# A graph attention layer on one core: a 23rd key-and-value buffer, and the running of the segment maxima one step later

## The chip, the core and the metric

The kernel runs on one core of a Trainium2 chip. A core has five instruction queues that run side by side[...]: TensorE (PE in the profile, with its weight loads as PEld), VectorE (DVE), ScalarE (ACT), GpSimd (POOL) and SyncE (SP, which here only issues DMAs). The metric is device time in microseconds (us) of one launch; lower is better.

## The reference

There are 3125 nodes with 128 features, and 100,000 edges, sorted by destination, each of one of 5 types. For every type r the edges of that type attend, per destination node and head (8 heads of 16):

```python
logits = (q * k).sum(-1) / scale + attn_bias[r][None, :]
masked_logits = jnp.where(mask[:, None], logits, NEG)
max_v = jax.ops.segment_max(masked_logits, dst, num_segments=n)
exp_l = jnp.where(mask[:, None], jnp.exp(masked_logits - max_v[dst]), 0.0)
sum_exp = jax.ops.segment_sum(exp_l, dst, num_segments=n)
attn = exp_l / (sum_exp[dst] + 1e-12)
out = out + jax.ops.segment_sum(attn[:, :, None] * v, dst, num_segments=n)
```

Here q comes from the destination's features, k and v from the source's, with weights of the type. The sum over the types goes through an output projection, is added to the features and normalised, added to the features once more and normalised again.

## The kernel before

**Tables.** A prologue (about the first 120 us) multiplies the features with the weights of keys and values of all types and stores them in DRAM as `kv_d`, one row of 256 floats per node and type. Queries go to `q_d`, three bf16 parts each.

**Groups and steps.** The edges are cut into 196 groups of 512 (4 tiles of 128). A group's edges touch at most 25 consecutive nodes, so 125 rows of node and type. The main loop runs over steps k. In a step, group k goes through the first half of the work (logits), and an older group v, 16 to 19 steps behind (19 from v = 22 on), goes through the second half (softmax weights and sums). Keys and values of a group stay in SBUF in between: `kvs_[g % KVB]`, with KVB = 22 buffers of 4 KB per partition.

**The loop's operations**, by the names in the code and the line that the profile shows:

- `gather(g)` (L681, POOL): four indirect DMAs, each fetching 128 rows of `kv_d`. It is called AHEAD = 2 steps before the group's logits: in step k for group k + 2. It writes the buffer that group k + 2 - 22 read last in `weigh`.
- `spread_q` (L746, PE): one-hot matrix `hot` times the queries, 12 bf16 matmuls. `logits` (L759 product, L760 sum, DVE); `store_logits` (L765, SP) puts them in `lg_d`. `spot` (L737, DVE) makes `hot` for a later group from `kt`, which `fetch_keys` (L367, SP) brings; `fetch_q` (L373, SP) brings `qw`. Both are issued three steps ahead.
- `fetch_m` (L853, SP) brings the maxima `mw` of group v; `spread_m` (L863, PE) spreads them over the edges, into `me`; `less_max` (L872, DVE) subtracts; `exps` (L876, ACT); `weigh` (L881, DVE) multiplies the values; `weights` (L889, ACT); `sums` (L915, L917, L924, PE) adds up per node and type; `norm` (L936 to L939, DVE) divides.

On DVE the order within step k is `weigh(v)`, `less_max` of the next v, `norm`, `logits(k)`, `spot`, then parts of queries, maxima, projection and norms where they are due. On PE it is `spread_m` of the next v, `sums`, `spread_q(k+1)`. Each queue runs strictly in this written order.

**The maxima.** Nodes are handled in blocks of 128 (25 blocks, about 8 steps apart). `full_step[b]` is the step after whose logits all edges of block b have theirs; `ready[b]` is 8 steps later for whole blocks (7 for the last, smaller one), and is the first step in which a group of block b may be in its second half. In between:

- step ready - 7: `maxima_load` (L772, POOL), an indirect DMA from `lg_d` into `ell`. It waits for the last `store_logits` of the block to have landed, and gathers stand behind it in POOL's queue.
- steps ready - 6, - 5 and - 4, at the end of the step on DVE: `maxima` in three parts, for types 0 and 1, 2 and 3, and 4 (L795, L805, L810, L816; with the last part L821 to L831). The first part begins with an ACT copy `by_head` (L787). The last, smaller block does all in one part at ready - 4.
- step ready - 3, early in the step on SP: `store_m` (L839), into `m_d`.
- step ready - 2: the first two `fetch_m` of the block (L853), which wait for that store.
- step ready - 1: PE's `spread_m` of the block's first group.

Every engine's program is in the order in which the Python calls are made (`tc.manual_schedule()`), and the waits follow from which buffers are written and read.

Of the kernel before, what the change touches and what calls it, by code (L numbers as in the profile page):

```python
# [59 lines left out]
SB = P * E // N // SR  # L60
SPAD = 5
QB = 3
KVB = 22
HELD = 21
KVA = 9

# [63 lines left out]
NM = len(MB)  # L130


def windowed_path(
# [539 lines left out]
    ps = ctx.enter_context(tc.tile_pool(name="ps", bufs=2, space=PSUM))  # L673
    buffers(i for i in range(KVB) if i not in at_once)
    hold = ctx.enter_context(tc.tile_pool(name="hold", bufs=HELD))
    flow = ctx.enter_context(tc.tile_pool(name="flow", bufs=2))
    late_flow = ctx.enter_context(tc.tile_pool(name="late_flow", bufs=2))
    def gather(g):
        kv = kvs_[g % KVB]
        for t in range(T):  # L680
# [75 lines left out]
    def logits(g):  # L756
        kv, lg = kvs_[g % KVB], live["lg", g]
        prod = flow.tile([P, T, H], F32, name="prod", bufs=1)
# [20 lines left out]
    def maxima(b, c0, c1):  # L779

        whole = MB[b][2] is None
        nh = HEADS if whole else HEADS // 2
        if c0 == 0:
            ell = live.pop(("ell", b))
            by_head = ps.tile([P, HEADS, D], F32, name="by_head", bufs=1)[:, :nh]
            if whole:
                nc.scalar.copy(by_head, ell[:, :, :HEADS].rearrange("p s k -> p k s"))  # L787
            else:
                for h in range(2):
                    at = slice(h * P // 2, (h + 1) * P // 2)  # L790
                    nc.scalar.copy(
                        by_head[at], ell[at, :, h * nh : (h + 1) * nh].rearrange("p s k -> p k s")
                    )
            mine = late_flow.tile([P, D], F32, name="mine", bufs=1)
            nc.vector.scalar_tensor_tensor(  # L795
                mine, slot, deg[:, b : b + 1], ell[:, :, HEADS], op0=ALU.is_lt, op1=ALU.mult
            )
            mx = late_flow.tile([P, R, HEADS], F32, name="mx", bufs=1)
            mx = mx.rearrange("p r k -> p (r k)")[:, : R * nh].rearrange("p (r k) -> p r k", k=nh)
            live["max", b] = by_head, mine, mx  # L800
        by_head, mine, mx = live["max", b]
        n = c1 - c0
        shut = late_flow.tile([P, R, D], F32, name="shut", bufs=1)
        for r in range(c0, c1):
            nc.vector.tensor_scalar(  # L805
                shut[:, r - c0, :], mine, float(r + 1), -BIG, op0=ALU.not_equal, op1=ALU.mult
            )
        wl = late_flow.tile([P, RH * HEADS, D], F32, name="wl", tag="wl", bufs=1)
        wl = wl[:, : n * nh].rearrange("p (r k) s -> p r k s", k=nh)
        nc.vector.tensor_tensor(  # L810
            wl,
            by_head[:, None].to_broadcast([P, n, nh, D]),
            shut[:, :n, None, :].to_broadcast([P, n, nh, D]),
            op=ALU.add,
        )
        nc.vector.tensor_reduce(mx[:, c0:c1], wl, AX.X, ALU.max)  # L816
        if c1 < R:
            return
        live.pop(("max", b))
        bias = bias4 if whole else bias_h  # L820
        nc.vector.tensor_tensor(mx, mx, bias, op=ALU.add)  # L821
        nc.vector.scalar_tensor_tensor(mx, mx, NEG4, bias, op0=ALU.max, op1=ALU.subtract)
        m3 = late_flow.tile([P, R, 2, 3, HEADS // 2], BF16, name="m3")
        if whole:
            mxs = mx.rearrange("p r (h k) -> p r h k", h=2)
        else:
            m3, mxs = m3[:, :, :1], mx[:, :, None, :]
        nc.vector.tensor_copy(m3[:, :, :, 0, :], mxs)
        nc.vector.tensor_tensor(mxs, mxs, m3[:, :, :, 0, :], op=ALU.subtract)
        nc.vector.tensor_copy(m3[:, :, :, 1, :], mxs)  # L830
        nc.vector.tensor_tensor(m3[:, :, :, 2, :], mxs, m3[:, :, :, 1, :], op=ALU.subtract)  # L831
        live["m3", b] = m3

    def store_m(b):
        n0, n1, part = MB[b]
        m3 = live.pop(("m3", b))
        to = m_d[n0 * R : (n0 + (P if part is None else P // 2)) * R, :]
        if part is None:
            nc.sync.dma_start(  # L839
                to.rearrange("(p r) c -> p (r c)", r=R), m3.rearrange("p r h s k -> p (r h s k)")  # L840
            )
        else:
            to = to.rearrange("(p r) (h c) -> h p r c", r=R, h=2)
            for h in range(2):
                nc.sync.dma_start(
                    to[h],
                    m3[h * P // 2 : (h + 1) * P // 2, :, 0].rearrange("p r s k -> p r (s k)"),
                )
# [176 lines left out]
    def lag(b):  # L1025

        return LAG if MB[b][2] is None else LAG_H

    full_step = [step_of[full_at(n, D)] for n in MEND]
    ready = [full_step[b] + lag(b) for b in range(NM)]  # L1030


    at_k, k = {}, 0
    for v in range(NGR):
        k = max(k + 1, ready[block_of(v, MEND)])
# [26 lines left out]
    for k in range(-2, root_at[NT] + 2):  # L1062
        v, g = v_at.get(k), group_at.get(k)
        q_step = {k - f: b for b, f in enumerate(q_from) if b >= QB and -2 <= k - f <= 5}

        if k >= 0 and k + 3 in group_at:
            fetch_keys(group_at[k + 3])
            fetch_q(group_at[k + 3])
        if -2 in q_step:
            fetch_x("xq", q_step[-2])  # L1070
        for b in range(NT):
            if done_at[b] - 1 == k:
                fetch_x("xr", b)
            if norm_at[b + 1] + 1 == k:
                store_z(b)
        for b in range(NM):
            if ready[b] - 3 == k:
                store_m(b)
        if 5 in q_step:
            store_q(q_step[5])  # L1080
        for u in range(NGR):
            if max(at_k[u] - 3, ready[block_of(u, MEND)] - 2) == k:
                fetch_m(u)

        while gathered < NGR - 1 and step_of[gathered + 1] <= k + (AHEAD if k < final - 16 else 1):
            gathered += 1
            gather(gathered)
        for b in range(NM):
            if full_step[b] + 1 == k:
                maxima_load(b)  # L1090

        for b in range(NT):
            if done_at[b] + 1 == k:
                residual(b)
        if v_at.get(k - 4) is not None:
            by_node(v_at[k - 4])
        if v_at.get(k - 2) is not None:
            carry(v_at[k - 2])
        if 1 in q_step:
            turned(q_step[1])  # L1100
        if 3 in q_step or 4 in q_step:
            second_part()
        if 2 in q_step or 3 in q_step:
            first_part()

        if v_at.get(k + 1) is not None:
            spread_m(v_at[k + 1], 8 if k + 1 in group_at else 12)
        if v_at.get(k - 1) is not None or v_at.get(k - 3) is not None:
            sums(v_at.get(k - 1), v_at.get(k - 3))
        if k + 1 in group_at:  # L1110
            spread_q(group_at[k + 1])

        if v is not None:
            weigh(v)
        if v_at.get(k + 1) is not None:
            less_max(v_at[k + 1])
            exps(v_at[k + 1])
        if v is not None:
            weights(v)
        if k + 1 in group_at:  # L1120
            types(group_at[k + 1])
        if v_at.get(k - 2) is not None:
            norm(v_at[k - 2])
        if g is not None:
            logits(g)
            store_logits(g)
        if k + 2 in group_at:
            spot(group_at[k + 2])
        if v_at.get(k + 1) is not None:
            places(v_at[k + 1], 2 if k >= final - 1 else 0)  # L1130
        if 3 in q_step or 4 in q_step:
            third_part()
        if 2 in q_step or 3 in q_step:
            remainder()
        for b in range(NM):
            whole = MB[b][2] is None
            if ready[b] - 6 == k and whole:
                maxima(b, 0, 2)
            if ready[b] - 5 == k and whole:
                maxima(b, 2, 4)  # L1140
            if ready[b] - 4 == k:
                maxima(b, 4 if whole else 0, R)
        for b in range(NT):
            if done_at[b] == k:
                project(b)
        for b in range(NT + 1):
            if root_at[b] == k:
                roots(b)
            if norm_at[b] == k:
                norms(b)  # L1150
        if 0 in q_step:
            turn_q(q_step[0])
        if 1 in q_step:
            queries(q_step[1], 0, RH)
        if 2 in q_step:
            queries(q_step[2], RH, R)
# [505 lines left out]
```

## Time and profile before

| what | value |
|---|---|
| three runs | 1645.75, 1625.92, 1644.51 us; median 1644.51 |
| the profiled execution's own time | 1596.71 us |
| its span in the profile | 1594.9 us |
| busy: PE, DVE, ACT, POOL | 978.5, 931.1, 636.1, 797.2 us |
| mean granted TensorE clock | 0.707 |
| DMA moved | 203.63 MB, 128 GB/s |
| eight steps (one block of nodes) in the middle of the loop | about 57 us |

No engine is busy for more than 61% of the span. Busy time is an average: the loop's steps are held up by waits, and the rows that name these waits are in the prediction. In the page's groups the columns are: line, engine, operation, what is written and read, count, busy us, mean ns, and the idle time of the engine just before these instructions with who ended most of it. "remote" stands for a release that the profile cannot name, "issue" for time in which the engine waited for nothing that the profile shows. Matmul ends are modelled; when a matmul was really done shows in when the engine that waits for it goes on.

### The profile page before, as it was taken

To read this page: it belongs to the slowest core of one execution; us is meant where nothing else is said; L and a number is where in the kernel's file an instruction comes from. 1 tells how busy PE (TensorE), PEld (TensorE's weight loads), DVE (VectorE), ACT (ScalarE), POOL (GpSimd) and SP (SyncE) were. 2 spreads that over 40 slices of the span, in tenths; PEclk is the share of its full clock that TensorE was granted. 3 is DMA by queue.
4 is the path that set the end of the run, shared out by engine and by line. 5 is a ranking of instruction groups with operands and counts; after the bars stand their busy time and mean duration, and the time that the engine had idled before them with its cause. 6 is when DMAs were issued, how large, how long until landed. Compare 5 with 4: busy or idle time off the path is not lost. (4 is left out here: it accounts for less than half of the span.)

```text
span 1594.9 us, 25686 instructions
## 1 busy us (share of the span) xinstructions
PE 978.5 (61%) x7526; PEld 752.9 (47%) x7526; DVE 931.1 (58%) x2559; ACT 636.1 (40%) x2248; POOL 797.2 (50%) x901
## 2 busy tenths in 40 slices
PE   7931423655676676667566657566676556565786
PEld 3520322434555554555454545455555444454664
DVE  5521623645756656656655656556665665664786
ACT  2620121324434444443453444343444344344454
POOL 3455446254555555555555555555555555455400
PEclk9965556766777767777776777676777777767678
DMA  6963634444545545555554554455555455444410
GB/s 191 357 195 97 153 85 128 103 109 122 139 120 128 144 121 121 138 131 122 119 132 105 133 136 121 117 133 123 129 138 133 111 138 134 111 127 119 102 27 15
DMA packets 180889, 203.63 MB, mean 128 GB/s; under 512 B 83207, under 2 KB 146083, under 8 KB 180620
## 3 DMA queue, kind: packets, MB, share of 16 engines
q0 software_dynamic: 40896, 113.39, 25.4%
q1 hardware_dynamic: 135414, 83.80, 23.4%
q10 hardware_dynamic: 4430, 4.71, 1.2%
q8 instruction: 63, 1.03, 0.3%
q14 instruction: 86, 0.70, 0.2%
HBM read 166.50 MB, written 35.28 MB: 127 GB/s over the span
## 5 line engine op out<-in xcount | busy, mean ns | idle before, releaser
L681 POOL DMA_INDIRECT kv<-kv_d,idx x784 | 742.5, 947 | 534.3 <-DVE den L936 252.9
L915 PE MATMUL pp<-wv,at 128*125 128x136 f32 x1568 | 399.6, 386 | 68.3 <-issue 62.1
L915 PEld LDWEIGHTS pp<-wv,at 128*125 128x125 f32 x1568 | 298.1, 256 | 154.8 <-issue 149.9
L746 PE MATMUL qe<-qw,hot 125*128 125x128 bf16 x2352 | 235.3, 261 | 139.9 <-issue 69.1
L863 PE MATMUL me<-mw,hot 125*128 125x64 bf16 (+1 forms) x2352 | 150.4, 217 | 237.5 <-issue 112.2
L746 PEld LDWEIGHTS <-hot 125*128 125x128 bf16 x2352 | 207.9, 127 | 158.4 <-issue 89.0
L872 DVE TENSOR_TENSOR me<-lg,me 128x32 f32<-128x32 f32 x196 | 37.8, 193 | 395.8 <-remote 247.0
L863 PEld LDWEIGHTS <-hot 125*128 125x128 bf16 x2352 | 130.9, 114 | 264.6 <-issue 232.9
L876 ACT ACTIVATE me<-me 128x32 f32<-128x32 f32 x196 | 35.7, 182 | 511.7 <-DVE me L872 318.6
L901 ACT ACTIVATE at<-row_at,nkey 128x125 f32<-128x125 f32 x744 | 237.5, 398 | 0.0
L759 DVE TENSOR_TENSOR prod<-kv,qe 128x512 f32<-128x512 f32 x196 | 132.8, 678 | 83.2 <-remote 62.1
L881 DVE TENSOR_TENSOR wv<-kv,me 128x512 f32<-128x512 f32 x196 | 132.8, 677 | 42.1 <-remote 32.6
L760 DVE TENSOR_REDUCE lg<-prod 128x32 f32<-128x512 f32 x196 | 134.4, 686 | 6.7
L904 ACT ACTIVATE at<-at 128x500 f32<-128x500 f32 (+1 forms) x196 | 117.4, 599 | 6.2
L917 PE MATMUL pp<-pt,carried 125*5 125x136 f32 x390 | 100.4, 346 | 30.7 <-issue 16.3
L707 PE MATMUL prq<-wq,xTq 128*128 128x384 f32 (+1 forms) x88 | 48.5, 639 | 81.0 <-DVE rem L717 59.9
L772 POOL DMA_INDIRECT ell<-lg_d,start_i x25 | 23.6, 945 | 149.1 <-DMA lg_d<-lg 52.4
L924 PEld LDWEIGHTS pp<-rsum,o 125*128 125x128 f32 x392 | 84.0, 258 | 18.7 <-issue 18.1
L949 ACT COPY oT<-pp 128x25 f32 x196 | 33.7, 172 | 135.9 <-remote 89.1
L810 DVE TENSOR_TENSOR wl<-by_head,shut 128x1024 f32<-128x1024 f32 (+2 forms) x73 | 76.9, 1053 | 17.2 <-issue 10.3
L924 PE MATMUL pp<-rsum,o 125*128 125x25 f32 x392 | 74.4, 270 | 18.3 <-issue 13.7
L816 DVE TENSOR_REDUCE mx<-wl 128x16 f32<-128x1024 f32 (+2 forms) x73 | 76.5, 1048 | 2.5
(184 smaller groups left out, 1018.6 us busy)
## 6 DMA issues: line engine op xcount, KB each, us to landing
kt<-key_d SPq DMA_DIRECT2D x196, 128.0 KB
qw<-q_d SPq DMA_DIRECT2D x196, 96.0 KB
kv_d<-kvs SPq DMA_DIRECT2D x24, 640.0 KB
kv<-kv_d,idx POOLq DMA_INDIRECT x784
q_d<-q SPq DMA_DIRECT2D x22, 480.0 KB
lg_d<-lg SPq DMA_DIRECT2D x196, 18.0 KB
mw<-m_d SPq DMA_DIRECT2D x196, 6.0 KB
xr<-in_x SPq DMA_DIRECT2D x24, 64.0 KB
```

What stands on the lines that cost most here:

```text
L681: nc.gpsimd.indirect_dma_start(out=kv[:, t, :], out_offset=None, in_=kv_d[:, :], in_offset=bass.IndirectOffsetOnAxis(ap=idx[:, t, g : g + ...
L746: nc.tensor.matmul(qe[:, t, :], hot[:, t, :], qw[:WR, s, :], start=(s == 0), stop=(s == 2))
L759: nc.vector.tensor_tensor(prod, kv[:, :, :H], live.pop(("qe", g)), op=ALU.mult)
L760: nc.vector.tensor_reduce(lg[:, :, :HEADS], prod.rearrange("p t (k d) -> p t k d", d=HD), AX.X, ALU.add)
L810: nc.vector.tensor_tensor(wl, by_head[:, None].to_broadcast([P, n, nh, D]), shut[:, :n, None, :].to_broadcast([P, n, nh, D]), op=ALU.add,)
L863: nc.tensor.matmul(me[:, t], hot[:, t, :], mw[:WR, None, :, s, :].to_broadcast([WR, times, 2, HEADS // 2]), start=(s == 0), stop=(s == 2),)
L881: nc.vector.tensor_tensor(wv[:, :, :H].rearrange("p t (k d) -> p t k d", d=HD), kv[:, :, H:].rearrange("p t (k d) -> p t k d", d=HD), live ...
L901: nc.scalar.activation(at[:, t, :], row_at[:, :WR], AF.Abs, bias=nkey[:, t, g : g + 1], scale=1.0)
L904: nc.scalar.activation(at[:, on_dve:], at[:, on_dve:], AF.Relu, bias=1.0, scale=-1.0)
L915: nc.tensor.matmul(pp, at[:, t, :], wv[:, t, :], start=(t == 0), stop=(t == T - 1))
L917: nc.tensor.matmul(pp[:R], carried[:WR, g, :], live.pop(("pt", g - 1)), start=False, stop=False,)
L924: nc.tensor.matmul(op, live.pop(("o5", done)), rsum[:WR], start=True, stop=True)
```

## The change

The number of buffers goes from 22 to 23, with AHEAD unchanged at 2. `last` is the step of a block's last part of the maxima: ready - 3 for whole blocks, ready - 4 as it was for the smaller one. The parts run in `last` - 2, `last` - 1 and `last`, so one step later than before for whole blocks. `store_m` is called right behind the last part, at the end of that step, where it was called early in step ready - 3. `maxima_load` (ready - 7) and `fetch_m` (ready - 2 at the earliest) stay where they were.

```diff
-KVB = 22
+KVB = 23
...
-        for b in range(NM):
-            if ready[b] - 3 == k:
-                store_m(b)
...
         for b in range(NM):
             whole = MB[b][2] is None
-            if ready[b] - 6 == k and whole:
+            last = ready[b] - (3 if whole else 4)
+            if last - 2 == k and whole:
                 maxima(b, 0, 2)
-            if ready[b] - 5 == k and whole:
+            if last - 1 == k and whole:
                 maxima(b, 2, 4)
-            if ready[b] - 4 == k:
+            if last == k:
                 maxima(b, 4 if whole else 0, R)
+                store_m(b)
```

## The prediction

> **What bounds the kernel now.** I read the groups first, for who waits for whom. Columns after the bar: busy us, mean ns, then idle time before with its releasers.
>
> ```profile
> L681 POOL DMA_INDIRECT kv<-kv_d,idx x784 | 742.5, 947 | 534.3 <-DVE den L936 252.9
> L872 DVE TENSOR_TENSOR me<-lg,me 128x32 f32<-128x32 f32 x196 | 37.8, 193 | 395.8 <-remote 247.0
> L863 PE MATMUL me<-mw,hot 125*128 125x64 bf16 (+1 forms) x2352 | 150.4, 217 | 237.5 <-issue 112.2
> L772 POOL DMA_INDIRECT ell<-lg_d,start_i x25 | 23.6, 945 | 149.1 <-DMA lg_d<-lg 52.4
> ```
>
> DVE's great idle time stands in front of `less_max`, 395.8 of its 664 idle us: it waits for PE's `spread_m`. POOL's 534.3 us in front of gathers are waits for a buffer, released by DVE. DVE hardly waits for gathers: between the last issue of a group's gather and its product (L759) lie 12 to 26 us in steps 42 to 177 (I took the difference of the two rows for each group).
>
> Why does PE keep `less_max` waiting? The timeline (start us, duration) of POOL and of DVE early in the loop shows it most plainly:
>
> ```profile
> 242.88 0.94 POOL L772 DMA_INDIRECT ell<-lg_d,start_i  x1 [22.59 <-DMA lg_d<-lg]
> 245.91 0.94 POOL L681 DMA_INDIRECT kv<-kv_d,idx  x1 [2.09 <-issue]
> ...
> 279.66 0.94 POOL L681 DMA_INDIRECT kv<-kv_d,idx  x1 [0.30 <-issue]
> 291.70 0.94 POOL L681 DMA_INDIRECT kv<-kv_d,idx  x1 [11.09 <-DVE den L936]
> ```
>
> ```profile
> 260.16 0.69 DVE L881 TENSOR_TENSOR wv<-kv,me 128x512 f32<-128x512 f32 x1 [3.29 <-remote]
> 285.51 0.20 DVE L872 TENSOR_TENSOR me<-lg,me 128x32 f32<-128x32 f32 x1 [24.66 <-remote]
> ```
>
> From 245.9 to 280.6 POOL issues 28 gathers without a pause, 1.25 us each; DVE stands from 261 until 285.5, when PE has at last delivered. In the middle of the loop it is the same on a smaller scale:
>
> ```profile
> 680.05 0.68 DVE L881 TENSOR_TENSOR wv<-kv,me 128x512 f32<-128x512 f32 x1
> 683.42 0.68 DVE L881 TENSOR_TENSOR wv<-kv,me 128x512 f32<-128x512 f32 x1
> 691.03 0.20 DVE L872 TENSOR_TENSOR me<-lg,me 128x32 f32<-128x32 f32 x1 [6.93 <-remote]
> ```
>
> ```profile
> 681.00 0.94 POOL L681 DMA_INDIRECT kv<-kv_d,idx  x1 [3.90 <-DVE den L936]
> ...
> 689.75 0.95 POOL L681 DMA_INDIRECT kv<-kv_d,idx  x1 [0.30 <-issue]
> 695.29 0.94 POOL L681 DMA_INDIRECT kv<-kv_d,idx  x1 [4.59 <-DVE den L936]
> ```
>
> Two `weigh` free two buffers, POOL gathers two groups from 681.0 to 690.7, and `less_max` goes on at 691.03, 0.3 us after the last of them. So a step costs the 5 us of its gathers, in which PE delivers little after the first one or two us, and some 2.2 us in which PE and DVE catch up. A typical block of eight steps is 57.2 us: 40 of gathers, 1.25 for `ell`, 16 of POOL's pauses. I call the time in which PE delivers nothing the freeze; the trace does not say by what way a gather causes it.
>
> A rule of the Trainium skill speaks against this reading: "Trainium Architecture — The Big Picture", section "What this means for kernel authors", holds the engines for independent processors that delay one another through semaphores alone. `spread_m` waits for no gather. By the rule a longer run of gathers costs nothing, and the sum below would be -4 us at most. I go by the rows. Another, "Perfetto Trace Analysis", section "Optimization Strategy", says that a gap repeating on the engine that should be saturated can mean too few buffers. That reading of the 534.3 us would promise a gain from buffer 23; with 12 us of lead at least, POOL isn't that engine, and I put its worth at nothing.
>
> **Buffer 23.** The same 784 gathers of 0.947 us, no instruction added. `gather` in step k now needs the `weigh` of step k - 2, not k - 1. In steady running one `weigh` still frees one group. What changes is the meeting with `ell` once a block: POOL comes to it a step earlier, waits longer, and then finds three groups freed at once. I walk one block with the durations of 680 to 725, step 78 (third part included, see below) to 84, where the logits of step 81 close a block.
> - Before: `weigh` of 78 and 79 at 680.05 and 683.42; gathers to 690.7; `weigh` of 80 and 81 at 694.34 and 699.00; gathers 695.29 to 704.97; `less_max` of 81 at 706.08; `ell` 710.49; `weigh` of 83 at 711.47; gathers 711.74 to 721.44; `weigh` of 84 at 723.29, 1.85 after their end.
> - After: `weigh` of 78 at 680.05 frees a group, 681.0 to 685.7. Step 78 now holds the third part of the maxima, 3.0 us, so `weigh` of 79 is at 686.6 and frees the next, 687.6 to 692.3; that of 80, at about 690.3, the third, to 697.0. POOL then stands at `ell`, and nothing freezes: `less_max` of 80 about 697.8, `weigh` of 81 701.6, product of 81 703.1 (before 706.8), `ell` 3.7 later as before, 706.8, `weigh` of 83 at 707.7. Three groups are free: gathers from 708.0 to 723.0, where two ended at 721.44. `weigh` of 84 follows 1.85 later, 724.9 against 723.29.
>
> So DVE is 3.7 us ahead at `ell` and loses it all in the longer run: +1.6 us a block. The trace also has a stretch with that slack: steps 26 to 42, whose groups have a lag of 18 and not 19. From product 26 to product 42 it takes 120.6 us (305.5 to 426.1), and its `ell` waits 11.2 and 14.4 us, against 0.3 to 5.9 later. Two typical blocks take 114.4: +3.1 us a block. Against it stand steps 178 to 194, with one step of AHEAD and so the same slack: 105.6 us, but without new queries. That bounds it below, at about -3. I take +1.8, near the walk: 19 blocks from step 42, **+34**.
>
> **The maxima one step later.** Per block the same four L810/L816 pairs of 0.7 to 1.23 us and the tail L821 to L831, some 8.5 us, in other steps of DVE. The step in which the norms are due (717.1 to 722.2 in the timeline) loses 3.4 us of maxima; that time lay in a freeze, so it returns nothing. In the last of the three steps 3.0 us come before the next `weigh`; the walk has that. What waits for `ell` now is small: 10.2 us before `by_head` and 8.5 before `mine` in the whole run. A step later they are gone; half lies elsewhere hidden: **-4**.
>
> **The store at the end.** One DMA of 30 KB per block on SP. Before, it stood ahead of step ready - 3's `store_logits`; now SP waits for DVE's third part, about 3.7 us behind the `store_logits`. Behind it are queued the next `fetch_keys` and `fetch_q` (used 13 us after issue, covered) and the first two `fetch_m`. SP needs 3.4 us from the first of these to the first `mw` (682.97 to 686.38), and PE's weight load follows 2.55 us later. So `mw` comes some 4 us later: 692.9 in the walk, while `less_max` of 80 is held to 697.8 by gathers. Without that cover PE would wait 2.6 to 4 us a block. At the end of the loop there are no gathers left to cover it, and steps are short: two blocks, **+5**.
>
> Sum: 34 - 4 + 5 = +35 on 1596.71, or 2.2%. The profiled execution is 2.9% faster than the median of the runs, so I carry the ratio over: 1644.5 x 1.022 = **1680**.
>
> **Rivals.**
> - *Faster: more gathers under DVE work.* A single group's run beside a step with 5 to 6 us of DVE work costs POOL only a 0.93 us pause (the row at step 84), where runs of two cost 4.4 for two (my mean over 31 of them). Norms and maxima no longer share a step, so four steps of a block could cover a group, not three. Two more such groups save 2 x 1.3 us a block, 21 blocks: -55 us, 3.4%: 1588. It decides if the runs stay single; against it, the longer wait at `ell` makes runs of three.
> - *No change.* The time gained before `ell` and lost behind it are equal, as blocks of 52 and 63 us that follow each other already show: 1640 to 1650.
> - *Clearly slower: the maxima's store.* If the freeze ends before `mw` lands, PE waits up to 4.2 us in each of 22 blocks: +92 us, 1740. For it: in 10 of 22 blocks the first `spread_m` starts right behind its weight load, so `mw` is what came last. Against: DVE needs its result 3.3 us later.
>
> **The numbers.** A measurement of this kernel can tell about 2%. Forecast (slower by 2 to 4.5%, its own range 1660 to 1715) 0.33; no change 0.32; faster 0.25; clearly slower 0.10. So faster 0.25, same 0.32, slower 0.43. The range takes in half of the faster case and most of the slow one: 1600 to 1735.
>
> **What would show it.** `ell`'s idle time grows from 149 us to some 230 and is released by the store of the logits; gathers come in runs of 12 behind it; `less_max` keeps 380 to 430 us of idle time; PE's waits for `mw` stay below 40 us. I am wrong if POOL's runs become single and `less_max` waits under 330, or if `less_max` no longer follows the end of a run.

## The result and the profile after

| what | before | after |
|---|---|---|
| median of the runs | 1645.13 us (1625.92 to 1645.93, 4 runs) | 1742.81 us (1739.17 to 1749.28, 4 runs) |
| profiled execution | 1596.71 us | 1749.28 us |
| product of step 0 to that of step 42 | 304.1 us | 314.6 us |
| steps 42 to 178 | 982.0 us | 1100.2 us |
| steps 178 to 195, and from there to the end | 111.9 and 74.8 us | 128.9 and 78.3 us |

The ratio is 1.0656 with a 95% interval of 1.0603 to 1.0709: slower by 6.6%. The execution of the kernel before that left the trace, 1596.71 us, was faster than any of its four runs, so the two traces lie 153 us apart where the medians lie 98. They show where the time went, but make its amounts too large. Nearly all of it lies in the loop, and 118 us in its middle, where a block of eight steps grew from 57.8 to 64.7 us.

The rows of the groups after the change, columns as before:

```profile
L681 POOL DMA_INDIRECT kv<-kv_d,idx x784 | 745.1, 950 | 511.3 <-issue 225.9
L872 DVE TENSOR_TENSOR me<-lg,me 128x32 f32<-128x32 f32 x196 | 37.7, 192 | 547.9 <-remote 410.1
L863 PE MATMUL me<-mw,hot 125*128 125x64 bf16 (+1 forms) x2352 | 139.6, 219 | 186.6 <-ACT wv L889 72.5
L772 POOL DMA_INDIRECT ell<-lg_d,start_i x25 | 23.6, 943 | 318.4 <-DMA lg_d<-lg 146.3
```

The operations of POOL and DVE in these rows kept their length. POOL's idle time before `ell` more than doubled (149.1 to 318.4 us), and DVE waits 152 us more in front of `less_max` (395.8 to 547.9), about as much as the span grew. The timeline of one block shows how the two belong together. DVE first, `weigh` (L881) and `less_max` (L872):

```profile
565.03 0.65 DVE L881 TENSOR_TENSOR wv<-kv,me 128x512 f32<-128x512 f32 x1
...
567.91 0.68 DVE L881 TENSOR_TENSOR wv<-kv,me 128x512 f32<-128x512 f32 x1
...
570.82 0.68 DVE L881 TENSOR_TENSOR wv<-kv,me 128x512 f32<-128x512 f32 x1
...
576.49 0.68 DVE L881 TENSOR_TENSOR wv<-kv,me 128x512 f32<-128x512 f32 x1
595.75 0.20 DVE L872 TENSOR_TENSOR me<-lg,me 128x32 f32<-128x32 f32 x1 [18.59 <-remote]
```

And POOL in the same stretch:

```profile
571.51 0.94 POOL L772 DMA_INDIRECT ell<-lg_d,start_i  x1 [12.08 <-DMA lg_d<-lg]
572.76 0.95 POOL L681 DMA_INDIRECT kv<-kv_d,idx  x1 [0.30 <-issue]
...
591.53 0.95 POOL L681 DMA_INDIRECT kv<-kv_d,idx  x1 [0.30 <-issue]
602.50 0.95 POOL L681 DMA_INDIRECT kv<-kv_d,idx  x1 [10.02 <-DVE den L936]
```

POOL stands at `ell` for 12 us, up to 571.5. No gather runs, so DVE steps at 2.9 us a step and sets one buffer free with each `weigh`. When `ell` is out, POOL finds three groups free; the fourth `weigh` (576.49) is done 4.4 us after the first of their gathers has started. So POOL issues 16 gathers in 20 us, and the next one waits for the `weigh` behind them (602.5). `less_max` waits 18.6 us during that run and goes on 3.3 us after its last gather. Between steps 42 and 178 there are 17 such runs of four groups, one per block; before there was none (52 runs of one group, 41 of two, one of three; after 40, 14 and 17 of four. I join groups whose gathers follow each other within 0.8 us). All 17 stand right behind `ell`. In each of them DVE starts exactly one `weigh`, as it does in each of the 14 runs of two: a run twice as long brings DVE no further.

What PE does meanwhile, its matmuls in order of time:

```profile
577.33 0.33 PE L746 MATMUL qe<-qw,hot 125*128 125x128 bf16 x3
578.00 0.22 PE L746 MATMUL qe<-qw,hot 125*128 125x128 bf16 x1 [0.34 <-issue]
579.41 0.27 PE L746 MATMUL qe<-qw,hot 125*128 125x128 bf16 x1 [1.20 <-issue]
580.87 0.26 PE L746 MATMUL qe<-qw,hot 125*128 125x128 bf16 x1 [1.19 <-issue]
...
589.34 0.26 PE L746 MATMUL qe<-qw,hot 125*128 125x128 bf16 x1 [1.14 <-issue]
591.43 0.27 PE L746 MATMUL qe<-qw,hot 125*128 125x128 bf16 x1 [1.83 <-issue]
```

One `spread_q`, twelve matmuls that otherwise take 0.8 us, is drawn out over 14 us. Most of its matmuls start 1.4 us apart or a multiple of 0.7, with a weight load half-way between; the profile has no releaser for them ("issue"). So the freeze of the prediction is visible: PE waits for nothing that the profile shows, and crawls.

The crawl in these records is not the whole of it. Counted through the run, the `spread_m` that `less_max` waits for at 595.75 is this one:

```profile
574.39 0.52 PE L863 MATMUL me<-mw,hot 125*128 125x64 bf16 x12
```

It stands ahead of the crawl, and DVE got its result some 21 us after its modelled end. Whether PE works further behind than its records say, or the result was done and reached DVE late, no run shows.

### The profile page after: what moved, and what is told of

It is laid out like the page before. It is cut to its first block, busy times and chain, and to the rows that moved or that the text cites. A ratio compares the mean times of both kernels' runs of the same rounds, so it can differ in the third digit from the quotient of the medians.

```text
span 1747.5 us, 25673 instructions
## 1 busy us (share of the span) xinstructions
PE 988.0 (57%) x7526; PEld 749.7 (43%) x7526; DVE 928.0 (53%) x2559; ACT 629.9 (36%) x2248; POOL 799.9 (46%) x901
## 4 chain that ended last, share of the span: by engine, by line
DVE 26%; another core or an unknown queue 25%; PE 19%; issue 15%; ACT 6%; DMA 4%; POOL 2%; SPq 1%; DVEq 0%; ACTq 0%; POOLq 0%
PE pp L915 6%; DVE prod L759 4%; DVE wv L881 4%; DVE lg L760 3%; DVE wl L810 3%; PE qe L746 3%; PE pr L395 3%; PE me L863 3%; ACT at L901 2%; POOL kv L681 2%; DVE mx L816 2%; DVE hot L737 2%; PE pp L917 1%; DMA mw<-m_d 1%
## 5 line engine op out<-in xcount | busy, mean ns | idle before, releaser
L915 PE MATMUL pp<-wv,at 128*125 128x136 f32 x1568 | 392.8, 385 | 47.0 <-issue 45.0
L746 PE MATMUL qe<-qw,hot 125*128 125x128 bf16 x2352 | 255.4, 261 | 289.4 <-issue 250.3
L746 PEld LDWEIGHTS <-hot 125*128 125x128 bf16 x2352 | 208.9, 126 | 314.1 <-issue 274.1
L872 DVE TENSOR_TENSOR me<-lg,me 128x32 f32<-128x32 f32 x196 | 37.7, 192 | 547.9 <-remote 410.1
L863 PE MATMUL me<-mw,hot 125*128 125x64 bf16 (+1 forms) x2352 | 139.6, 219 | 186.6 <-ACT wv L889 72.5
L863 PEld LDWEIGHTS <-hot 125*128 125x128 bf16 x2352 | 124.9, 115 | 227.8 <-issue 191.2
L772 POOL DMA_INDIRECT ell<-lg_d,start_i x25 | 23.6, 943 | 318.4 <-DMA lg_d<-lg 146.3
L881 DVE TENSOR_TENSOR wv<-kv,me 128x512 f32<-128x512 f32 x196 | 132.7, 677 | 53.2 <-remote 40.1
L707 PE MATMUL prq<-wq,xTq 128*128 128x384 f32 (+1 forms) x88 | 54.5, 714 | 104.0 <-DVE hot L737 48.8
L737 DVE TENSOR_SCALAR hot<-kt,row_of 125x512 bf16<-125x512 bf16 x196 | 68.5, 350 | 3.8 <-DMA kt<-key_d 3.4
```

Of the source, the lines that this page charges most:

```text
L746: nc.tensor.matmul(qe[:, t, :], hot[:, t, :], qw[:WR, s, :], start=(s == 0), stop=(s == 2))
L863: nc.tensor.matmul(me[:, t], hot[:, t, :], mw[:WR, None, :, s, :].to_broadcast([WR, times, 2, HEADS // 2]), start=(s == 0), stop=(s == 2),)
L881: nc.vector.tensor_tensor(wv[:, :, :H].rearrange("p t (k d) -> p t k d", d=HD), kv[:, :, H:].rearrange("p t (k d) -> p t k d", d=HD), live ...
L915: nc.tensor.matmul(pp, at[:, t, :], wv[:, t, :], start=(t == 0), stop=(t == T - 1))
```

## The experiments

Each kernel ran on one chip together with the kernel before, and each ratio is to the kernel before on that chip. The chips differ: they run the kernel before in 1586, 1630, 1249, 1580 and 1631 us. The one of 1249 us is a case of its own, see below. Of the kernel before there is one trace, so what is compared with it below is mostly from another chip.

### The two parts alone, and the buffer's effect undone (before: 1586 us)

`kvb_alone` is the kernel before with one edit, `maxima_alone` the changed kernel with the opposite one:

```diff
-KVB = 22
+KVB = 23
```

> The kernel before with 23 buffers, maxima and store left where they were. Theory 1 (the buffer: POOL meets the maxima's load a step earlier, stands there some 12 us while DVE frees four buffers, and then gathers four groups in one run): 1720 to 1750 us, nearly all of the change's +98; POOL's idle time before the load of ell about 320 us, about 17 runs of four groups in the loop's middle. Theory 2 (the maxima and their store a step later: PE waits for mw, DVE's third part stands in the way): 1635 to 1655 us, PE's wait for mw stays near 14 us.

> The changed kernel with 22 buffers again; the maxima a step later and the store at their end stay. Theory 1: 1635 to 1660 us, ell's idle time near 150 us, runs of gathers of one and two groups; PE's wait for mw may be 30 to 60 us but is covered by runs of gathers. Theory 2: 1720 to 1745 us, with less_max released by what follows mw.

`ahead3` is the changed kernel with gathers three steps ahead; `ell_later` has `maxima_load` one step later in POOL's program:

```diff
-AHEAD = 2
+AHEAD = 3
```

```diff
-            if full_step[b] + 1 == k:
+            if full_step[b] + 2 == k:
```

> The changed kernel with gathers three steps ahead instead of two, so that buffer 23 is used and a gather again needs the weigh of the step just before. Theory 1: 1635 to 1665 us, since POOL meets ell one step later in terms of weigh, as before; ell idle 130 to 200 us, hardly any run of four. Theory 2: 1720 to 1745 us, as in the changed kernel.

> The changed kernel with the load of ell one step later in POOL's program, where the parts of the maxima now have a step to spare. Theory 1: 1630 to 1665 us: POOL reaches ell one group of gathers later, ell's idle time falls from 318 us to 200 or less and the runs of four go. Theory 2: 1720 to 1745 us, with the wait for mw as in the changed kernel (about 55 us).

| kernel | ratio, 95% interval | idle before `ell` | runs of 1, 2, 3, 4 groups |
|---|---|---|---|
| kvb_alone | 1.047 (1.039 to 1.055) | 243.5 us | 35, 17, 1, 16 |
| maxima_alone | 1.022 (1.013 to 1.030) | 131.8 us | 58, 18, 14, 0 |
| ahead3 | 1.021 (1.011 to 1.031) | 138.7 us | 58, 17, 15, 0 |
| ell_later | 1.023 (1.015 to 1.031) | 139.8 us | 56, 17, 15, 0 |

Each theory had one part right. The buffer alone brings the runs of four and 4.7%; the maxima and their store bring another 2.2%. The product of the two, 1.0468 x 1.0215 = 1.069, lies within the interval of the change's ratio; on another chip the change cost 8.0% (`after_2`, below), so that the parts simply multiply is likely and not settled. `ahead3` keeps 23 buffers, and `ell_later` keeps them and the two steps of lead: in both the runs of four are gone and with them the buffer's cost, and what remains is that of `maxima_alone`. So it is not the buffer that costs but the distance between POOL and DVE at the moment when POOL stands at `ell`.

One row misleads here. `less_max`, which grew by 152 us with both parts, did not grow with either alone: 393.6 us in `kvb_alone` and 393.9 in `maxima_alone`, against 395.8. In `kvb_alone` DVE waits longer elsewhere, most of all 41.4 us in front of `h` (L976, before 17.3), which also needs PE. The trace before is from another chip than these two.

### Is the freeze real, and what makes it (before: 1630 us)

`half_rows` moves half the bytes with the same instructions; `plain_rows` moves the same bytes by plain DMAs from the same queue:

```diff
-                out=kv[:, t, :], out_offset=None, in_=kv_d[:, :],
+                out=kv[:, t, :H], out_offset=None, in_=kv_d[:, :],
...
-            kv[:, :, H:].rearrange("p t (k d) -> p t k d", d=HD),
+            kv[:, :, :H].rearrange("p t (k d) -> p t k d", d=HD),
```

```diff
-            nc.gpsimd.indirect_dma_start(
-                out=kv[:, t, :], out_offset=None, in_=kv_d[:, :],
-                in_offset=bass.IndirectOffsetOnAxis(ap=idx[:, t, g : g + 1], axis=0),
-            )
+            at = (g * 61 + t * 17) % (15000)
+            nc.gpsimd.dma_start(kv[:, t, :], kv_d[at : at + P, :])
```

> The kernel before, in which a gather fetches only the first half of each row (the keys, 64 KB instead of 128 KB) and weigh multiplies the keys in place of the values; the values are left out, all instructions stay in number and order. Theory T (the bytes that move slow PE down): ratio below 0.90, PE's records 0.70 us apart nearly gone. Theory P (it is POOL's making of 128 indirect descriptors that PE feels, whatever they carry): ratio 0.97 to 1.01, slow stretches as long as before.

> The kernel before, in which each of POOL's four DMAs of a group fetches 128 consecutive rows by a plain DMA instead of 128 rows by index: same bytes, same queue, the indices left out. Theory T (bytes): within 3% of the kernel before. Theory P (the indirect operation): ratio below 0.90, and less_max's idle time below 200 us. If POOL's issue of a plain DMA is itself slow for PE, it stays within 3% as by T, and half_rows tells the two apart.

`half_rows`: 1.015 (1.006 to 1.024). `plain_rows`: 0.736 (0.731 to 0.742), 1202 us. The groups of `plain_rows`:

```profile
L682 POOL DMA_DIRECT2D kv<-kv_d x784 | 418.5, 546 | 436.9 <-DVE den L934 317.9
L870 DVE TENSOR_TENSOR me<-lg,me 128x32 f32<-128x32 f32 x196 | 37.6, 192 | 85.9 <-PE me L861 81.3
```

and of `half_rows`:

```profile
L681 POOL DMA_INDIRECT kv<-kv_d,idx x784 | 743.5, 948 | 601.5 <-DVE den L936 289.4
L872 DVE TENSOR_TENSOR me<-lg,me 128x32 f32<-128x32 f32 x196 | 37.7, 192 | 413.9 <-remote 228.8
```

The plain DMA takes 546 ns instead of 947, but POOL did not bound the loop: what falls is `less_max`'s wait, to 85.9 us, and what is left has a releaser with a name, PE. A count says the same: between steps 42 and 178, successive PE instructions (weight loads included) start 0.64 to 0.76 us apart (I call these slow starts) 178 times in the trace before, 164 times in `half_rows` and 3 times in `plain_rows`. So it is the indirect gathers that slow PE, and not the bytes that they move. `plain_rows` changes three things at once, though: no index is read, the 128 rows are consecutive, and POOL is busy for less time. Which of them it takes was not tested.

Two more kernels on this chip. `kvb21` has one buffer fewer and calls `gather` behind `weigh`:

```diff
-KVB = 22
+KVB = 21
...
+        while gathered < NGR - 1 and step_of[gathered + 1] <= k + (AHEAD if k < final - 16 else 1):
+            gathered += 1
+            gather(gathered)
```

(the same lines, and `maxima_load` behind them, are taken away from the head of the step). `store_late` only moves `store_m`, still at ready - 3, from the head to the end of its step:

```diff
-        for b in range(NM):
-            if ready[b] - 3 == k:
-                store_m(b)
...
+        for b in range(NM):
+            if ready[b] - 3 == k:
+                store_m(b)
         for b in range(NT):
             if done_at[b] == k:
                 project(b)
```

> The kernel before with 21 buffers, one fewer, the gather called behind weigh in its step, since it now needs the weigh of its own step. Theory R (the number of buffers sets how many groups are free at once when POOL leaves ell; long runs of gathers cost PE more than short ones): ratio 0.97 to 1.00, runs of one group, ell's idle time under 100 us. Rival (buffers are lead, and 22 was just enough): ratio 1.01 to 1.04, gathers single but each waiting for DVE, less_max's idle time above 430 us.

> The kernel before, with only the maxima's store moved to the end of step ready - 3; the three parts stay in their steps, 22 buffers. Theory S (mw comes late to PE because the store is issued late): ratio to the kernel before 1.01 to 1.025, PE's wait for mw 40 to 80 us instead of 14. Theory D (what the move of the maxima costs is DVE's third part standing in step ready - 3): ratio 0.995 to 1.007, and mw still early enough, since the store no longer waits for DVE.

`kvb21`: 1.010 (1.003 to 1.017). The runs are 97 of one group and 20 of two, `ell`'s idle time 86.8 us, and it is no faster: each single group now waits for its own step's `weigh` (POOL's idle time before gathers 644.7 us). The theory that fewer free groups are simply better is wrong; 22 was better than 23, and by 1% than 21. The rival's sign, over 430 us in front of `less_max`, did not come either: 404.9. `store_late`: 1.001 (0.997 to 1.004), PE's wait for `mw` 14.4 us. The store's place at the end of the step costs nothing by itself, as long as it doesn't wait for DVE.

### What the maxima's move costs

`third_first` puts the third part and the store at the head of DVE's step ready - 3; `two_parts` leaves the last part in ready - 4 and has only two:

```diff
+        for b in range(NM):
+            if ready[b] - 3 == k and MB[b][2] is None:
+                maxima(b, 4, R)
+                store_m(b)
         if v is not None:
             weigh(v)
...
-            if last == k:
-                maxima(b, 4 if whole else 0, R)
+            if last == k and not whole:
+                maxima(b, 0, R)
                 store_m(b)
```

```diff
-            if ready[b] - 6 == k and whole:
-                maxima(b, 0, 2)
             if ready[b] - 5 == k and whole:
-                maxima(b, 2, 4)
+                maxima(b, 0, 2)
             if ready[b] - 4 == k:
-                maxima(b, 4 if whole else 0, R)
+                maxima(b, 2 if whole else 0, R)
```

`early_store` adds to `two_parts` the store right behind the last part and a `fetch_m` three steps ahead of use for every group:

```diff
-            if max(at_k[u] - 3, ready[block_of(u, MEND)] - 2) == k:
+            if at_k[u] - 3 == k:
                 fetch_m(u)
...
                 maxima(b, 2 if whole else 0, R)
+                store_m(b)
```

`first_stays` is `maxima_alone` with the first part back in ready - 6; `early_parts` is the kernel before with types 2 to 4 together in ready - 5:

```diff
-            if last - 2 == k and whole:
+            if last - 3 == k and whole:
                 maxima(b, 0, 2)
```

```diff
             if ready[b] - 5 == k and whole:
-                maxima(b, 2, 4)
-            if ready[b] - 4 == k:
-                maxima(b, 4 if whole else 0, R)
+                maxima(b, 2, R)
+            if ready[b] - 4 == k and not whole:
+                maxima(b, 0, R)
```

> maxima_alone (22 buffers, maxima a step later) with the third part of the maxima and the store behind it moved to the head of DVE's step ready - 3, before weigh. Theory L (what the move of the maxima costs is that mw is late: the store waits for the third part, and PE waits for mw): mw is some 6 us earlier, PE's wait for it falls from 82 us to under 30, ratio to the kernel before 0.995 to 1.01. Theory D (it is the 3 us of DVE work in that step, which hold up a weigh and with it a gather): ratio 1.015 to 1.03 as in maxima_alone, whatever the wait for mw.

> The kernel before with the maxima in two parts: types 0 and 1 in step ready - 5, types 2 to 4 in step ready - 4; the store stays early in step ready - 3. So the first part comes a step later, as in the change, and the last does not. Theory L (late mw): ratio 0.99 to 1.007, PE's wait for mw near 14 us. Theory D' (the first part's place, or DVE's work bunched in fewer steps, is what costs): ratio 1.015 to 1.03.

> third_first again (22 buffers, maxima a step later, third part and store at the head of DVE's step ready - 3). On a chip of about 1600 us: theory L (mw late) ratio 0.99 to 1.01; theory D (DVE's 3 us in that step) 1.015 to 1.03. On a chip of about 1250 us: 0.965 to 0.98, as measured.

> two_parts again (types 0 and 1 in step ready - 5, types 2 to 4 in ready - 4, store as before). On a chip of about 1600 us: theory L 0.985 to 1.007; theory D' (bunched work, first part late) 1.015 to 1.03. On a chip of about 1250 us: 0.96 to 0.975, as measured.

> two_parts with the store right behind the last part, at the end of step ready - 4, and fetch_m of a block's first group three steps ahead of its use instead of two. If PE's wait for mw bounds anything, this removes it (under 10 us) and gains 1 to 2% on two_parts; if PE waits for something else anyway, it is within 0.5% of two_parts.

> 22 buffers; the first part of the maxima stays in step ready - 6, the second and third come in ready - 4 and ready - 3 and the store at the end of ready - 3, as in the change. On a chip of about 1600 us: if the place of the first part is what costs, ratio 0.99 to 1.01; if the two later parts or the store are, 1.015 to 1.03 as in maxima_alone. PE's wait for mw is near 80 us in both cases.

> The kernel before with the maxima in two parts, types 0 and 1 in step ready - 6, types 2 to 4 in ready - 5; store as before. On a chip of about 1600 us: if the place of the first part is what costs, ratio 0.98 to 1.01; if three types in one step cost (as they may in two_parts), 1.02 to 1.035.

| kernel | ratio, 95% interval | PE's wait for `mw` | kernel before |
|---|---|---|---|
| third_first | 0.971 (0.965 to 0.977) | 83.6 us | 1249 us |
| two_parts | 0.965 (0.960 to 0.971) | 85.8 us | 1249 us |
| third_first_2 | 1.040 (1.031 to 1.048) | 17.7 us | 1580 us |
| two_parts_2 | 1.033 (1.028 to 1.038) | 15.6 us | 1580 us |
| early_store | 1.025 (1.016 to 1.033) | 7.7 us | 1580 us |
| first_stays | 1.024 (1.014 to 1.034) | 60.0 us | 1631 us |
| early_parts | 1.034 (1.023 to 1.044) | 33.9 us | 1631 us |

The wait is a line of the view of `spread_m`'s line in the code (us, times); it stands so in `maxima_alone`

```profile
  DMA mw<-m_d: 82.5, 30
```

in `third_first_2`

```profile
  DMA mw<-m_d: 17.7, 8
```

and in `early_store`

```profile
  DMA mw<-m_d: 7.7, 4
```

On the chips of about 1600 us three theories fall one after the other. Late `mw`: three kernels have PE's wait under 18 us (14.3 before) and are 2.5 to 4.0% slower all the same. The third part in ready - 3: `two_parts_2` and `early_parts` have none there. The first part in ready - 5: `first_stays` has it in its old place. `early_store` gains 0.7% on `two_parts_2`, with which it shares all but store and `fetch_m`: between the 1 to 2% expected if the wait for `mw` bounds and the 0.5% if it doesn't, and far from the whole cost. Each of the four placings of the same 8.5 us of DVE work in this table costs 2.4 to 4.0%, and that of `maxima_alone` 2.2%. What these kernels share in their traces is 6 to 18 runs of three groups between steps 42 and 178 (before 1, `store_late` 3). That is a common sign, not a cause shown: what the 2.2% of the maxima's move come from is left open.

### The chip on which PE does not stand still

`third_first`, `two_parts` and two others ran on the chip that runs the kernel before in 1249 us. The groups of `third_first` there:

```profile
L681 POOL DMA_INDIRECT kv<-kv_d,idx x784 | 747.8, 954 | 255.4 <-issue 196.4
L872 DVE TENSOR_TENSOR me<-lg,me 128x32 f32<-128x32 f32 x196 | 37.6, 192 | 97.0 <-PE me L863 96.1
```

A gather takes as long as elsewhere, 954 ns. But POOL issues eight groups without a pause, 42 us, and DVE goes on beside it; `less_max` waits 97 us in all. POOL is the bound there (1.25 us a gather, 5.3 us a step), and the placings that lose elsewhere gain 3%. The count of PE's slow starts is 4 in `third_first` and 7 in `two_parts`; the same two kernels have 157 and 158 on the chip of 1580 us.

`after_plain` is the changed kernel with the edit of `plain_rows`. `paused` is the kernel before with four `iota` of 0.24 us into an unused tile ahead of each group's gathers:

```diff
         kv = kvs_[g % KVB]
+        for _ in range(4):
+            nc.gpsimd.iota(rest, pattern=[[1, P]], base=0, channel_multiplier=0, allow_small_or_imprecise_dtypes=True)
```

> The changed kernel with each gather replaced by a plain DMA of 128 consecutive rows, as plain_rows has it for the kernel before; the indices are left out. Theory F (both parts of the change cost through PE's standing still in runs of indirect gathers): the buffer's 4.7% is gone, ratio to the kernel before 0.73 to 0.75, within 2% of plain_rows (0.736). Theory W (the change costs through waits that have nothing to do with how a gather is made, at ell and for mw): 5 to 7% above plain_rows, a ratio of 0.77 to 0.79.

> The kernel before with four small POOL operations (some 0.9 us in all, into a tile that nothing reads) ahead of each group's gathers, so that two groups never follow without a pause. If PE catches up in such a pause, runs of two cost less than now: ratio 0.95 to 0.99, less_max's idle time under 350 us. If PE needs over a microsecond after the last gather before it runs again, the pause is only added to POOL's time: ratio 1.00 to 1.06.

`after_plain`: 1211.7 us, 0.971 (0.963 to 0.978) of the kernel before with its gathers on that chip. My expectation had counted on a base of 1600 us, so the ratio itself answers nothing. In absolute time it is 0.8% above `plain_rows`, which ran on another chip; as far as two chips can be compared, the 6.6% are gone with the indirect gathers, although POOL still waits 316.7 us for `ell`. `paused`: 1.176 (1.169 to 1.183), outside both expectations; with no freeze to shorten, the pause is only added to the time of POOL, the bound there, so it says nothing of the chips that have a freeze.

`after_2`, the changed kernel once more, ran on the chip of 1580 us:

> The changed kernel once more, beside the others of this call. On a chip that runs the kernel before in about 1600 us: ratio 1.06 to 1.07 as measured. On one that runs it in about 1250 us, theory F (the change costs only through PE standing still in long runs of gathers): ratio 0.96 to 1.00; theory W (waits at ell and for mw cost by themselves): 1.03 or more.

1.080 (1.074 to 1.085), more than the 1.06 to 1.07 expected: again 17 runs of four groups, a block of 62.7 us, `ell` 311.8 us, `less_max` 528.0 us. What the change does on the chip of 1249 us was not run.

## Why the prediction was wrong

**Direction right, size wrong.** The forecast was slower by 2.2%, from POOL meeting `ell` a step early and a longer run of gathers behind it. That is what the trace shows. But 1742.81 lies above the range: two terms of the sum were too small, the buffer's +34 and the +1 of the maxima and their store.

**The freeze.** Seen in every trace with indirect gathers from the chips of about 1600 us (113 to 243 slow starts). The rule that engines delay each other through semaphores alone (the Trainium skill, "Trainium Architecture — The Big Picture", "What this means for kernel authors") would have promised -4 us at most; with the indirect gathers replaced, `less_max`'s wait fell to 85.9 us from the 395.8 of the trace before (another chip), though `spread_m` waits for no gather, so a coupling without a semaphore exists here. On the chip of 1249 us the rule's picture fits.

**The step that failed first: the walk's three groups freed at once, +1.6 us a block, +1.8 taken.** The walk put the next `weigh` (that of 84) 1.85 us behind the run's end, as in the trace before. But there DVE's own work held it: from 714.80 to 722.2 DVE is busy with hardly a pause, with a product, the first part of the maxima and the norms, and waits only 1.13 us after that.

```profile
721.85 0.32 DVE L1007 TENSOR_SCALAR z<-y,mv,sd 128x128 f32<-128x128 f32 x1
723.29 0.69 DVE L881 TENSOR_TENSOR wv<-kv,me 128x512 f32<-128x512 f32 x1 [1.13 <-remote]
```

With DVE earlier at `ell`, this `weigh` falls into the run and sets a fourth group free: in the 17 runs of four of the changed kernel it is done 3.4 to 14.5 us after the first gather's start, most often 4 to 5, in the 16 of `kvb_alone` mostly 9 to 11. In `kvb_alone` the maxima are still in that step, so the fourth group goes with or without them.

In size: alone the buffer costs 4.7%, some 74 us on its chip, where the sum had 34 us or 2.1%. The profiled execution of `kvb_alone` is 57 us longer than that of the kernel before, on another chip: 36 between steps 42 and 178 (1017.8 against 982.0 us, where 17 blocks of 1.8 had made 31), and 21 before step 42 and from 178 to 195, where the sum had 4. So as far as these two traces can be compared, more was missed at the start and the end of the loop than in its middle; the sum had nothing for the start. Its `ell` waits 243.5 us, near the 230 predicted for the whole change.

**The second failing term: the maxima -4 and the store +5.** Together they cost 2.2%, about 34 us, where +1 was predicted. I had priced the moved work as if a freeze covered it wherever it stands; the measured 2.2% show that it does not, and what they come from stays open. The experiments show that it is not the store's place nor `mw` alone. The rival that gave 1740 us was near the measured time by luck: its reason was the wait for `mw`. PE's wait for `mw` did grow, to 54.7 us where under 40 was predicted:

```profile
  DMA mw<-m_d: 54.7, 22
```

but shortening it bought nothing that brings a kernel back to 1.00.

**The signs.** `ell` released by the store of the logits: right, at 318 us instead of 230. Runs of three groups: four. `less_max` at 380 to 430 us: 547.9.

**The rival "faster"** needed runs that stay single; 40 of 71 runs are, but each block pays for them with a run of four. The reading of a repeating gap as too few buffers (the Trainium skill, "Perfetto Trace Analysis", "Optimization Strategy") is meant for the engine that should be saturated; the prediction held that POOL isn't that engine, and the 4.7% that buffer 23 cost agree. `kvb21` says that taking one away is no cure.

## What to carry to other kernels

When a queue waits at one place once per period, count how many requests the other side completes during that wait: one more buffer lets them all go at once, and if the burst slows a third engine, slack is paid for and not gained. A schedule can be tuned to its own stalls: here each of five other placings of one piece of work cost 2 to 4% where gathers slow PE, while two of them gained 3% where they don't. So measure a schedule on more than one chip before its order is trusted.

## What the runs showed of the hardware

- While POOL issues indirect DMAs back to back, PE's instructions start 0.70 us apart or a multiple of it, in the run of the timeline above from about 5 us after its first gather until 1 us after its last one ended, in turn a weight load and a matmul. Half the bytes change nothing of it (164 slow starts against 178); plain DMAs of the same bytes end it (3). By what way they are coupled, no run shows.
- The granted clock sinks along with it, by the table of stretches (columns: stretch, length, busy us and count of PE, PE's weight load, DVE, ACT and POOL, then granted clock, DMA share, GB/s):

```profile
572.00:576.00 4.00, 2.89 (x36) 2.37 (x36) 3.06 (x11) 3.93 (x13) 3.08 (x4) 1.00 0.78 195
576.00:580.00 4.00, 1.61 (x11) 0.88 (x11) 1.13 (x4) 0.47 (x3) 3.06 (x4) 0.81 0.68 179
580.00:592.00 12.00, 1.85 (x7) 0.73 (x7) 0.00 (x0) 0.00 (x0) 8.98 (x10) 0.50 0.42 120
596.00:608.00 12.00, 10.31 (x74) 8.07 (x73) 11.23 (x26) 6.31 (x24) 3.79 (x4) 0.59 0.31 73
```

  Seven matmuls in 12 us at 0.50, and 74 in 12 us at 0.59 once the run is over: the low clock doesn't explain 0.70 us per instruction. It may be a result of PE's idleness, which was not tested. Mean clock 0.68 after, 0.80 in `plain_rows`.
- The kernel before took 1249 us on one chip and 1580 to 1645 on the others, a difference far larger than the change's. In `third_first`, traced on both kinds, the gathers are equally long and PE's slow starts are 4 against 157. Why the chips differ is open.
